# A two-layer convolution block on one core: four groups instead of three, with the last group kept on chip

## The chip, the cores and the metric

The kernel runs on one core of one Trainium2 chip. The metric is device time in microseconds, as the median of several runs of the whole kernel. A profile is one further execution with every engine's instructions, semaphores and DMA packets recorded. The engines are called PE (TensorE; PEld is its loading of weights), DVE (VectorE), ACT (ScalarE), POOL (GpSimd) and SP (the engine whose queue issues most DMAs here). ACTq, SPq and so on are the sequencers of these engines, which issue DMAs and wait.

## The reference

The input is 32 batches of 32 channels of 128x128 matrices in fp32. Two residual layers follow each other. `_gn` is a group norm over 16 groups of two channels.

```python
def layer0(A):                     # a matrix square root by iteration, for each of the 1024 matrices
    normA = sqrt(sum(A * A)); Y = A / normA; Z = I
    for _ in range(5):
        T = 0.5 * (3.0 * I - Z @ Y); Y = Y @ T; Z = T @ Z
    return Y * sqrt(normA)

def layer1(x, w1, w2):             # a spectral convolution
    X = fftn(x, axes=(2, 3)).real
    out = zeros
    out[:, :, :32, :32] = einsum('bixy,ioxy->boxy', X[:, :, :32, :32], w1)
    out[:, :, -32:, :32] = einsum('bixy,ioxy->boxy', X[:, :, -32:, :32], w2)
    return ifftn(out, axes=(2, 3)).real

x = x + layer0(_gn(x))
x = x + layer1(_gn(x), w1, w2)
```

## The kernel before, in words

**Layer 0 runs in sets.** A set is four channels of one batch, so a batch has 8 sets and there are 256. `newton` (L388) takes a set through its matrix products: `products` (L295, L298) makes four 128x128 products into one PSUM bank, `transposed` (L301, L304) makes four transposes on PE, `plus` (L270, L273) and `taken` (L262, L267) bring results out on DVE and ACT. At the end L410 adds the result to the input on DVE. There are two kinds of sets. For the far ones (batches 1 to 19, `is_far`, L307) `quartic` (L351) transposes by way of DVE and DRAM (L360 to L376); for the near ones (batch 0 and batches 20 to 31) it transposes on PE. Far sets may hold up to seven lanes at a time, near sets four, and a new set starts every 20/7 (far) or 13/4 (near) rounds (`LANES`, `LESS`, `FAR`, `NEAR`, L39 and L40).

**After a set** `settle` (L416) stores it to DRAM (`mid`, L418), folds its two halves on POOL (L423) and takes statistics on DVE (L427). After each four sets `forward` (L431) does the first transform. When a batch is complete, `spectrum` (L470) does the second transform (L479), then the group norm's statistics of the batch (`moments`, L493 to L516), then scales the spectrum (L521, L527) and stores it to DRAM (`xs`, L533).

**Layer 1 runs in groups of batches** (`GROUPS`, L41: 21, 8 and 3). When the last batch of a group has its spectrum, `follow` (L851) starts the products with the layer's weights for the whole group and puts the group's inverse transforms behind them. The first group uses `wide_products` (L540), where the weights stand on a diagonal in SBUF. Groups of at most eight use `small_products` (L596): the spectra are loaded onto the diagonal of two zeroed tiles (`diag0`, `diag1`, loads L617), the weights come in 16 steps of 512 KB (L611, L878), each step is 32 matmuls (L647), a pair of steps is copied out of PSUM (L662) and stored to DRAM (`od`, L626). A group with fewer than eight batches copies and stores four separate row ranges (`parts`, L600), alternately on ACT and DVE. `inverse` (L720) loads a batch's products (L683), reorders them on ACT for the small groups (`ob`, L730), transforms back on PE (L742, L764), copies parts on ACT (L748, L776), adds on DVE (L781) to the batch loaded from `mid` (L698), unfolds on POOL or in the tail partly on DVE (L717), and stores the output (L706).

**The order of work** is written out by hand: the loop at L868 makes rounds; in each round the lanes advance one stage and the generator queues `norms`, `preps`, `posts` (after a set), `specs` (spectra), `prods` (products) and `backs` (inverses) are stepped. `step` (L803) takes the first generator one stage on; when it has ended, it is removed and the next one waits for the next call. `backs` is stepped in four of five rounds, in every round once more than 26 batches have started to end. The framework that records the program orders each engine's instructions by its own priorities, except those wrapped in `kept`, which stay in program order; all engines execute in order.

**Tail.** `tail` is true when no set is left. Before, the tiles of the sets are then released (L875) and a pool `late` takes their place: 14 steps' weights for the last group are loaded there by POOL's queue (L878), and more room for `yt` tiles. Layer 0's buffers for far sets are given up once 20 batches have settled (`FIRST`, L50; `change`, L123), for the tiles of layer 1.

Of the kernel before, what the change touches and what calls it, by code (L numbers as in the profile page):

```python
# [26 lines left out]
F32 = mybir.dt.float32  # L28
# [12 lines left out]
GROUPS = (21, 8, 3)  # L41
# [8 lines left out]
FIRST = GROUPS[0] - 1  # L50
# [15 lines left out]
def conv_preact_kernel(  # L66
# [33 lines left out]
    for i, n in enumerate(GROUPS):  # L100
        few = n <= NB
        shape = [KK // 2, P, n, 64] if few else [KK, P, B, 32]
        xs.append(dram.tile(shape, F32, name=f"xs{i}", tag=f"xs{i}"))
        shape = [KK, 4, 32, 8 * C] if few else [KK, 4, B, L * C]
        od.append(dram.tile(shape, F32, name=f"od{i}", tag=f"od{i}"))
# [6 lines left out]
    phase = ctx.enter_context(ExitStack())  # L112
    sets = phase.enter_context(tc.tile_pool(name="sets", bufs=1))
# [356 lines left out]
    def spectrum(b, u, st):  # L470


        uv = u.rearrange("h s (t e l) c -> h s e t (l c)", e=2, l=4)
        ps = [bank() for _ in range(2)]
        for s in range(2):
            for i in range(2):
                for e in range(2):
                    rows = slice(64 * i, 64 * i + 64)
                    nc.tensor.matmul(  # L479
                        ps[i][64 * e : 64 * e + 64, 0:2, :],  # L480
                        tab[rows, T_FH.start + s * K : T_FH.start + (s + 1) * K],
                        uv[rows, s, e],
                        start=(s == 0),
                        stop=(s == 1),
                    )
        z = sp.tile([P, 4, P], F32, tag="sp", name="z", bufs=2)
        for i in range(2):
            nc.scalar.copy(
                z.rearrange("p t (l i c) -> p (t l) i c", i=2, c=G)[:, :, i, :],
                ps[i].rearrange("p a x -> p (a x)")[:, 0:256].rearrange("p (m c) -> p m c", c=G),  # L490
            )
        yield
# [23 lines left out]
        nc.vector.reciprocal(r, s)  # L516
        yield
        ps = transposed(z)
# [12 lines left out]
        i, j = where[b]  # L531
        kept(
# [63 lines left out]
    def small_products(i):  # L596

        n = GROUPS[i]

        parts = [slice(32 * q, 32 * q + 4 * n) for q in range(4)] if n < NB else [slice(0, P)]  # L600
        size = 4 * n * 64
        xks = [
            t[:, size * j : size * j + size].rearrange("p (b m) -> p b m", m=64)
            for t in diags
            for j in range(2048 // size)
        ]
        wts = [t.rearrange("p (e q t o) -> p e q t o", e=2, q=4, t=4) for t in plain] + late_wts

        def load_weights(kk):
            if kk < 2 or not late:  # L610
                kept(nc.sync.dma_start(out=wts[kk % len(wts)], in_=wk[kk]))  # L611

        def load_spectra(k2):
            for l4 in range(4):
                rows = slice(32 * l4, 32 * l4 + 32)
                kept(
                    nc.sync.dma_start(  # L617
                        out=xks[k2 % len(xks)][rows, n * l4 : n * l4 + n, :],
                        in_=xs[i][k2, rows, 0:n, :],
                    )  # L620
                )

        def store(k2, om):
            for rows in parts:
                kept(
                    nc.sync.dma_start(  # L626
                        out=od[i][2 * k2 : 2 * k2 + 2].rearrange("e q b x -> (q b) e x")[rows],
                        in_=om.rearrange("p (e x) -> p e x", e=2)[rows],
                    )
                )  # L630

        for t in diags:
            nc.gpsimd.memset(t, 0.0)
        for kk in range(2):
            load_weights(kk)
        for k2 in range(len(xks)):
            load_spectra(k2)
        done = None
        for kk in range(KK):
            yield  # L640
            k2, e = divmod(kk, 2)
            wt, xk = wts[kk % len(wts)], xks[k2 % len(xks)]
            if not e:
                pm = bank()
            for t in range(8):
                for q in range(4):
                    nc.tensor.matmul(  # L647
                        pm[32 * q : 32 * q + 4 * n, 2 * e + t // 4, 32 * (t % 4) : 32 * (t % 4) + 32],
                        xk[:, :, 32 * e + 8 * q + t],
                        wt[:, t // 4, q, t % 4, :],  # L650
                        start=True,
                        stop=True,
                    )
            if kk + len(wts) < KK:
                load_weights(kk + len(wts))
            if done and not e:
                store(*done)
            if e:
                om = page(f"om{i}_{k2}")[:, 0:512]
                for j, rows in enumerate(parts):  # L660
                    copy = nc.vector.tensor_copy if j % 2 else nc.scalar.copy
                    copy(om[rows], pm.rearrange("p a x -> p (a x)")[rows])  # L662
                done = k2, om
                if k2 + len(xks) < KK // 2:
                    load_spectra(k2 + len(xks))
        store(*done)
        yield

# [17 lines left out]
    def load_input(b, e):  # L686
# [4 lines left out]
        for i in range(2):  # L691
            o = 16 * e + 8 * i
            turn = len(yts) + i
            if late and turn % 2:
                y = late[0].tile([P, 8, P], F32, tag="yt_late", name=f"yt{b}_{o}", bufs=8)
            else:
                y = inv.tile([P, 8, P], F32, tag="yt", name=f"yt{b}_{o}", bufs=6)
# [105 lines left out]
    def step(queue):  # L803
        if queue and next(queue[0], queue) is queue:
            queue.pop(0)


    late = []
    late_wts = []
    lanes = [None] * LANES  # L810
# [19 lines left out]
    def end(b, g, xt):  # L830
# [6 lines left out]
        posts.append(settle(b, g, st, xt))  # L837
        if g % 4 == 3:
            posts.append(forward(b, g // 4, u))
        if g == C // 4 - 1:  # L840
            posts.append(last(b, u, st))

    def last(b, u, st):
        specs.append(spectrum(b, u, st))
# [23 lines left out]
    while todo or any(lanes) or posts or specs or prods or backs:  # L868
# [3 lines left out]
        if tail and not posts and not late:  # L872

            phase.close()
            late.append(ctx.enter_context(tc.tile_pool(name="late", bufs=1)))  # L875
            for kk in range(2, KK):
                late_wts.append(late[0].tile([P, 2, 4, 4, C], F32, name=f"wt{kk}_late"))
                nc.gpsimd.dma_start(out=late_wts[-1], in_=wk[kk])  # L878
        for i in range(LANES):
            step(norms)  # L880
            far = todo and is_far(todo[0][0])
            room = lanes[i] is None and (far or LANES - lanes.count(None) < LESS)
            if todo and room and rounds >= due:
# [6 lines left out]
                if stages:  # L890
                    stage()
            if lanes[i] is not None:
                b, g, xt, steps = lanes[i]
                if next(steps, lanes) is lanes:
# [10 lines left out]
            if i == 0 and (rounds % 5 or len(ended) > B - 6) or tail and not (posts or specs):  # L905
# [66 lines left out]
```

## Time and profile before

| what | us |
|---|---|
| median of 3 runs | 3214.82 |
| lowest and highest run | 3211.49 and 3221.01 |
| the profiled execution, its own time | 3217.96 |
| its span in the trace | 3216.0 |
| PE busy | 2973.3 |
| DVE busy | 2365.3 |
| POOL busy | 2008.4 |
| ACT busy | 1716.3 |

The span is from the first to the last record of the execution; its own time is measured from outside and has 1.96 us more. Busy time is the union of an engine's instructions. The page cuts the span in 40 slices and gives the busy share of each in tenths. Other views answer for a stretch of time: busy time of each engine, who waited for whom, the instructions in order of time, and the chain of work that ended last. Positions are microseconds from the start of the span. In the trace a matmul in fp32 with a moving operand has two records, a transpose has one; so `x64` on L647 is one step of 32 matmuls.

### The profile page before, as it was taken

The page shows a single profiled execution, that of the slowest core. Times are in us where ns is not written, and L with a number is a line of the kernel's source. Part 1 is how long each engine was busy: PE and PEld are TensorE (multiplying, and loading weights), DVE is VectorE, ACT ScalarE, POOL GpSimd, SP SyncE. Part 2 cuts the span into 40 slices and gives each one's busy share as a digit, 9 for nine tenths or more (in the row PEclk, how much of TensorE's full clock was granted, in tenths as well). Part 3 has the DMA queues.
Part 4 walks back from the last instruction along what each step waited for, and adds up shares of the span by engine and source line. Part 5 has one row for each costly group of instructions (what it writes and reads, how often), then busy time and mean ns, then how long its engine had stood idle before and what let it go on. Part 6 is the DMA issues. An engine that isn't in the chain of part 4 may idle for free.

```text
span 3216.0 us, 78946 instructions
## 1 busy us (share of the span) xinstructions
PE 2973.3 (92%) x29440; PEld 2836.6 (88%) x29440; DVE 2365.3 (74%) x5672; ACT 1716.3 (53%) x4148; POOL 2008.4 (62%) x2312
## 2 busy tenths in 40 slices
PE   6999999999999999999999999999999998999954
PEld 6889899899999999999999998898889888999853
DVE  5787788778888887888788665577767776756645
ACT  3555555565556655565565555455555544546533
POOL 3566666666767666666676553466767767746642
PEclk9999999999999999999999999999999999999975
DMA  3466566666666666666666336765767676576667
GB/s 122 148 190 190 192 201 202 186 199 204 196 208 200 210 191 196 207 204 200 191 211 193 96 96 207 227 214 185 232 201 243 213 240 208 193 225 209 207 238 255
DMA packets 482317, 637.55 MB, mean 198 GB/s; under 512 B 97936, under 2 KB 263056, under 8 KB 481936
## 3 DMA queue, kind: packets, MB, share of 16 engines
q1 hardware_dynamic: 366448, 413.30, 40.3%
q10 hardware_dynamic: 113472, 211.86, 21.1%
q0 software_dynamic: 2016, 7.34, 0.6%
q8 instruction: 235, 3.85, 0.5%
q14 instruction: 146, 1.20, 0.1%
HBM read 398.75 MB, written 233.57 MB: 197 GB/s over the span
## 4 chain that ended last, share of the span: by engine, by line
PE 67%; DVE 13%; DMA 12%; ACT 3%; issue 2%; POOL 1%; SPq 1%; ACTq 0%; DVEq 0%; POOLq 0%
PE ps L298 55%; PE ps L304 6%; DMA xs<-in_xt 5%; DMA turn<-turn 2%; PE ps L764 1%; DMA w<-turn 1%; DVE a_st L193 1%; PE ps L442 1%; DVE turn L360 1%; DVE q L273 1%; DVE yt L781 1%; DVE v L273 1%; PE ps L576 1%; PE ps L742 1%; DVE xt L410 1%
## 5 line engine op out<-in xcount | busy, mean ns | idle before, releaser
L298 PE MATMUL ps<-w,v 128*128 128x128 f32 x4096 | 548.5, 278 | 26.4 <-POOL w L376 14.1
L376 POOL TENSOR_TENSOR w<-w,r 128x512 f32<-128x512 f32 x304 | 386.7, 1275 | 270.5 <-DMA w<-turn 222.0
L298 PE MATMUL ps<-y,q 128*128 128x128 f32 x4096 | 549.6, 278 | 3.9 <-ACT y L267 2.2
L423 POOL TENSOR_TENSOR fold<-xt 128x256 f32<-128x256 f32 x512 | 363.7, 731 | 279.2 <-DVE xt L410 262.5
L328 ACT ACTIVATE b<-b,a_off,a_scr 128x128 f32<-128x128 f32 x1024 | 463.9, 489 | 129.7 <-issue 54.8
L298 PEld LDWEIGHTS ps<-w,v 128*128 128x128 f32 x4096 | 500.5, 193 | 35.2 <-POOL w L376 20.1
L298 PEld LDWEIGHTS ps<-y,q 128*128 128x128 f32 x4096 | 504.7, 194 | 7.0 <-ACT y L267 3.3
L273 DVE SCALAR_TENSOR_TENSOR q<-ps,eye 128x512 f32<-128x512 f32 x512 | 347.0, 678 | 99.5 <-PE ps L298 97.9
L717 POOL TENSOR_TENSOR yt<-yt,d 128x512 f32<-128x512 f32 x236 | 297.9, 1289 | 188.0 <-ACT d L776 155.0
L193 DVE BATCH_NORM_STATS2 a_st<-xs 128x6 f32<-128x128 f32 x1024 | 231.8, 279 | 143.4 <-DMA xs<-in_xt 143.0
L335 POOL TENSOR_SCALAR x<-xt,a_nm,a_sc 128x128 f32<-128x128 f32 x720 | 317.8, 454 | 23.9 <-DVE a_n L222 20.8
L404 ACT ACTIVATE y<-ps,a_t_s 128x128 f32<-128x128 f32 x1024 | 292.1, 369 | 62.3 <-PE ps L298 61.5
L292 POOL TENSOR_TENSOR r<-b,eye 128x512 f32<-128x512 f32 x104 | 132.8, 1277 | 283.8 <-issue 224.6
L298 PE MATMUL ps<-m,q 128*128 128x128 f32 x2048 | 280.3, 280 | 27.9 <-DVE q L273 27.6
L298 PE MATMUL ps<-m,mb 128*128 128x128 f32 x2048 | 282.4, 282 | 19.6 <-ACT mb L267 19.6
L273 DVE SCALAR_TENSOR_TENSOR v<-ps,x 128x512 f32<-128x512 f32 x256 | 175.5, 686 | 165.0 <-PE ps L298 162.9
L273 DVE SCALAR_TENSOR_TENSOR v<-ps,m 128x512 f32<-128x512 f32 x256 | 174.7, 683 | 162.8 <-PE ps L298 162.1
L298 PE MATMUL ps<-y,t 128*128 128x128 f32 x2048 | 280.6, 281 | 6.6 <-DVE t L273 4.5
L298 PEld LDWEIGHTS ps<-m,q 128*128 128x128 f32 x2048 | 252.1, 194 | 35.4 <-DVE q L273 17.9
L360 DVE STREAM_TRANSPOSE turn<-v 128x512 f32<-128x512 f32 x304 | 277.9, 914 | 7.2
L298 PE MATMUL ps<-x,b 128*128 128x128 f32 x2048 | 275.6, 278 | 5.6 <-POOL x L335 5.6
L298 PEld LDWEIGHTS ps<-m,mb 128*128 128x128 f32 x2048 | 254.9, 196 | 27.7 <-ACT mb L267 25.0
(124 smaller groups left out, 5867.6 us busy)
## 6 DMA issues: line engine op xcount, KB each, us to landing
turn<-turn SPq DMA_DIRECT2D x304, 256.0 KB
b<-in_x ACTq DMA_DIRECT2D x256, 256.0 KB
xt<-in_xt ACTq DMA_DIRECT2D x256, 256.0 KB
xs<-in_xt ACTq DMA_DIRECT2D x256, 256.0 KB
mid<-xt SPq DMA_DIRECT2D x256, 256.0 KB
yt<-mid SPq DMA_DIRECT2D x128, 512.0 KB
out<-yt SPq DMA_DIRECT2D x108, 512.0 KB
w<-turn SPq DMA_DIRECT2D x152, 256.0 KB
```

The costliest lines, as they stand in the source:

```text
L193: nc.vector.bn_stats(st[:, 4 * i + c, :], tiles[i][:, c, :])
L273: nc.vector.scalar_tensor_tensor(s, ps, f, t, ALU.mult, ALU.add)
L292: nc.gpsimd.tensor_tensor(r, mb, eye, ALU.add)
L298: nc.tensor.matmul(ps[:, j, :], lhsT[:, j], rhs[:, j], start=True, stop=True)
L304: nc.tensor.transpose(ps[:, j, :], t[:, j, :], ident)
L328: nc.scalar.activation(t, x, AF.Identity, bias=offset[:, c], scale=scale[:, c])
L335: nc.gpsimd.tensor_scalar(m[:, j, :], xt[:, j, :], nm[:, c // 2 : c // 2 + 1], sc[:, c : c + 1], ALU.add, ALU.mult,)
L360: nc.vector.transpose(blocks(t), v.rearrange(form, b=4))
L376: nc.gpsimd.tensor_tensor(w, w, r, ALU.add)
L404: nc.scalar.mul(y[:, j, :], py[:, j, :], sn[:, c : c + 1])
L423: nc.gpsimd.tensor_tensor(f[:, :, 64 * half : 64 * half + 64], xt[:, :, 0:64], xt[:, :, 64:128], op)
L717: engine.tensor_tensor(yh, yh, d, op)
```

## The change

The groups become 19, 8, 3 and 2, so batches 1 to 18 are far and 19 to 31 near. The group of three (batches 27 to 29) is treated before the last sets are through; the last group is batches 30 and 31. The last group (`own`) has no `xs` in DRAM: `spectrum` copies its scaled spectra straight onto the diagonal of `diag0` and `diag1`, in eight copies, four each on ACT and DVE. Those tiles are zeroed, and the weights of its first two steps loaded, at the end of the products of the group before. The other 14 steps' weights come as 28 half steps of 256 KB into tiles of the sets (tags b, x, xt, r, v, w) that the last sets no longer need; a generator `weights` issues them on SP once the last set has started, and after each stage of the last set and each settled set it can issue more. The pool `late` is gone; in the tail every third `yt` tile comes from the tag `fold`. In the last group four steps share one `om` page, so that there is half the number of stores, and the stores alternate between SP's and ACT's queue. The input of batch 30 is loaded at the start of its products.

The statistics of a batch become a generator of their own, `summed`, put ahead of the second `forward` of the batch. `step` goes on to the next generator in the same call when one has ended. `backs` is stepped in three of five rounds, and in every round once batch 31 has a set ended. Layer 0's far buffers are given up after 19 batches, the end of the first group.

```diff
-GROUPS = (21, 8, 3)
+GROUPS = (19, 8, 3, 2)
-FIRST = GROUPS[0] - 1
+FIRST = GROUPS[0]
...
-        xs.append(dram.tile(shape, F32, name=f"xs{i}", tag=f"xs{i}"))
+        if i < len(GROUPS) - 1:
+            xs.append(dram.tile(shape, F32, name=f"xs{i}", tag=f"xs{i}"))
...
+    def summed(b, st):
+        ms, _, d = yield from moments(st, "b")
...
+        scales[b] = v, r
+        yield
...
+        v, r = scales.pop(b)
         ps = transposed(z)
...
+        if i == len(xs):
+            n = GROUPS[i]
+            for e, t in enumerate(diags):
+                for l4 in range(4):
+                    rows = slice(32 * l4, 32 * l4 + 32)
+                    copy = nc.scalar.copy if l4 % 2 else nc.vector.tensor_copy
+                    copy(
+                        t.rearrange("p (k b m) -> p k b m", k=4, m=64)[rows, :, n * l4 + j, :],
+                        spec[rows, 8 * e : 8 * e + 8].rearrange("p (k e) q t -> p k (e q t)", e=2),
+                    )
+            yield
+            return
...
+            for j, rows in enumerate(parts):
+                queue = nc.scalar if own and j % 2 else nc.sync
                 kept(
-                    nc.sync.dma_start(
-                        out=od[i][2 * k2 : 2 * k2 + 2].rearrange("e q b x -> (q b) e x")[rows],
-                        in_=om.rearrange("p (e x) -> p e x", e=2)[rows],
+                    queue.dma_start(
+                        out=od[i][2 * k2 : 2 * k2 + held].rearrange("e q b x -> (q b) e x")[rows],
+                        in_=om[:, 0 : 256 * held].rearrange("p (e x) -> p e x", e=held)[rows],
                     )
                 )
...
+        held = 4 if own else 2
+        if not own:
+            for t in diags:
+                nc.gpsimd.memset(t, 0.0)
...
+        else:
+            for e in range(2):
+                load_input(B - n, e)
...
         store(*done)
+        if i == len(GROUPS) - 2:
+            for t in diags:
+                nc.gpsimd.memset(t, 0.0)
+            for kk in range(2):
+                load_weights(kk)
         yield
+
+    def weights():
+        kinds = [("b", 0)] * 5 + [("x", 0)] * 2 + [("b", 4)] + [("x", 4)] * 2
+        kinds += [("r", 9)] * 4 + [("v", 9)] * 3 + [("w", 9)] * 3
+        spent = 0
+        for half in range(4, 2 * KK):
+            while len(settled) - (B * C // 4 - 10) <= spent and (
+                not kinds or kinds[0][1] > len(stages_of_last)
+            ):
+                yield
+            if kinds and kinds[0][1] <= len(stages_of_last):
+                kind = kinds.pop(0)[0]
+            else:
+                kind = "xt"
+                spent += 1
+            t = four(kind, False)
+            late_wts.append(t)
+            kept(nc.sync.dma_start(out=t, in_=wk[half // 2, :, half % 2].rearrange("p q t o -> p q (t o)")))
+            yield
...
     def step(queue):
-        if queue and next(queue[0], queue) is queue:
+        while queue and next(queue[0], queue) is queue:
             queue.pop(0)
...
+        if g == C // 4 - 1:
+            posts.append(then(summed(b, st)))
         if g % 4 == 3:
             posts.append(forward(b, g // 4, u))
...
-        if tail and not posts and not late:
-            phase.close()
-            late.append(ctx.enter_context(tc.tile_pool(name="late", bufs=1)))
-            for kk in range(2, KK):
-                late_wts.append(late[0].tile([P, 2, 4, 4, C], F32, name=f"wt{kk}_late"))
-                nc.gpsimd.dma_start(out=late_wts[-1], in_=wk[kk])
...
-            if i == 0 and (rounds % 5 or len(ended) > B - 6) or tail and not (posts or specs):
+            if i == 0 and (rounds % 5 < 3 or len(ended) == B) or tail and not (posts or specs):
                 step(backs)
```

## The prediction

> **What bounds the kernel now.** I read the slices of the page first, then busy time by stretches, then the order of time after the last set of layer 0, then the chain for the price of single steps.
>
> The slices say where TensorE sets the pace and where it doesn't.
>
> ```profile
> span 3216.0 us, 78946 instructions
> PE   6999999999999999999999999999999998999954
> PEclk9999999999999999999999999999999999999975
> ```
>
> One slice is 80 us. TensorE is at nine tenths or more until the last two slices, where it is half idle and its clock falls. So there are two regimes. Until the last set of layer 0 ends (the last L410, at 3093.6) added TensorE work lengthens the span almost one for one; after it the time is a chain of hand-overs. The stretches give both their sizes (columns: stretch, length, then busy PE, PEld, DVE, ACT, POOL, then clock, DMA share, GB/s).
>
> ```profile
> 2100.00:2900.00 800.00, 751.68 (x7993) 712.12 (x7992) 572.18 (x1360) 405.59 (x989) 531.53 (x627) 0.98 0.65 214
> 2900.00:3093.60 193.60, 178.62 (x1792) 168.39 (x1794) 120.74 (x240) 105.86 (x237) 127.04 (x139) 0.97 0.65 202
> 3093.60:3109.00 15.40, 6.63 (x82) 4.55 (x74) 13.72 (x33) 6.93 (x16) 9.33 (x14) 0.80 0.90 300
> 3109.00:3127.90 18.90, 0.00 (x0) 0.03 (x1) 0.00 (x0) 0.00 (x0) 4.61 (x6) 0.50 0.91 357
> 3127.90:3167.10 39.20, 21.90 (x1088) 19.48 (x1088) 19.45 (x28) 12.86 (x26) 4.98 (x4) 0.59 0.58 184
> 3167.10:3181.20 14.10, 4.39 (x43) 4.10 (x46) 0.00 (x0) 3.93 (x4) 0.00 (x0) 0.50 0.80 216
> 3181.20:3211.40 30.20, 14.91 (x154) 13.09 (x153) 29.96 (x36) 12.03 (x30) 17.63 (x12) 0.56 0.96 337
> 3211.40:3216.00 4.60, 0.00 (x0) 0.00 (x0) 0.03 (x1) 0.00 (x0) 0.00 (x0) 0.50 0.57 228
> ```
>
> From 2900 to the last set TensorE idles 193.6 - 178.6 = 15.0 us. The tail is 122.4 us in six stretches, cut at events of the timeline:
>
> ```profile
> 3092.93 0.69 DVE L410 TENSOR_TENSOR xt<-ps,xt 128x512 f32<-128x512 f32 x1 [1.49 <-PE ps L298]
> ...
> 3109.02 0.37 SPq L533 DMA_DIRECT2D xs<-spec  x1
> ...
> 3127.90 1.90 PE L647 MATMUL ps<-plain,diag 128*12 128x32 f32 x128 [22.73 <-DMA diag<-xs]
> ...
> 3174.18 1.92 ACT L730 COPY ob<-or 128x1024 f32<-128x1024 f32 x1 [7.84 <-DMA or<-od]
> ```
>
> Spectrum of batch 31 (15.4), its way to DRAM and back (18.9, TensorE and VectorE idle), products (39.2, though TensorE works 21.9), products to DRAM, back and through the first transforms (14.1), three inverses in which VectorE is full (30.2), last stores (4.6).
>
> **What the Trainium skill says.** "DMA: Bandwidth & Descriptors", Anatomy of one DMA: a small transfer is mostly completion latency, about 2 us. The trace is worse: store and reload take 18.9 us, because the DMA share is 0.91 there (late weights and inputs run at the same time); so on-chip copies win the whole stretch. The same page, Issuing engines are not separate DMA queues: queues share 16 DMA engines, another queue saves issue time only. So moving the weights from POOL's queue to SP's changes no transfer, only who stands in line; an SP weight issue (L611) is 0.35 us. "TensorE: Matmul & The Clock Gate", Part 1: an idle array falls to half clock. The trace agrees (0.97 before the tail, 0.50 in the reload); I therefore leave the tail's matmuls at the tail's own rates.
>
> **The change, part by part.**
>
> *Tail, spectrum.* `summed` starts the statistics when the last set has settled, where before they stood behind `spectrum`'s matmuls and behind VectorE work of an inverse (L781 and L717, until about 3101.7). Timeline: last L410 to the u copies is 4.7 us (3093.6 to 3098.3). Then a short wait for the statistics 1.5, L479 1.1, z 0.7, transposes 1.1, spec 1.2, L527 0.2: 10.5 in place of 15.4. The instruction order has batch 29's VectorE adds before the last L410, so nothing else is in the way.
>
> *Tail, diagonal.* Eight copies of 32x256, four each on ACT and VectorE, replace store and load. No row has this form; ACT's 128x256 copy (L776) is 0.37, and "VectorE: DVE Perf Modes", The TRN2 errata, gives 224+256 cycles at 1.2 GHz = 0.40 us on ACT as an estimate. Side by side 1.5 us, one after another 3.2; I take 1.7, in place of 18.9. The memsets and the weights of the first two steps come earlier and are ready.
>
> *Tail, products.* In before each pair of steps waits on SP for a spectrum reload and four stores. After, no reloads, half as many stores on two queues. TensorE then sets the pace:
>
> ```profile
> 2864.72 1.07 PE ps L647 x63
> 2812.91 0.87 PE ps L304 x8
> 2946.52 1.09 PE ps L742 x16
> 2950.47 1.19 PE ps L764 x21
> ```
>
> (pieces of the chain: start, us). One step of products is 64 records, 1.07: 16 steps are 17.1. The last four copies alternate ACT and VectorE, 2.6 (3129.87 to 3132.50). 19.7 in place of 39.2; 22 if the copies of all eight pairs run one behind the other.
>
> *Tail, rest.* Products out and back I leave at 14.1 (12 to 16: both loads are issued at once, but share the queue). Two inverses instead of three, VectorE-bound at 30.2/3: 20.1. Last stores 4.6. The tail becomes 10.5+1.7+19.7+14.1+20.1+4.6 = 70.7; **saved 51.7** (46 to 58).
>
> *Main part, TensorE.* One more group means one more pass of products ahead of the last set: 17.1. Inverses are 32 either way; 30 are now done before the last set, where before it was 29 less half of one (L764 at 3099.7): 1.09+1.19+1.19 = 3.5, plus 1.2, together 4.7. Batch 19 changes from far to near: a near set transposes twice on TensorE (0.87, L304 x8) instead of by DMA; 8 sets are 7.0. Sum 28.8. If all 15 us of idle take some of it: 14; I take none, since those idle spots are late hand-overs that come with any inverse.
>
> *Main part, new waits.* (a) Group (27..29) has four separate row parts, so its copies alternate ACT, VectorE, ACT, VectorE (8 x 4) with work of the sets queued behind them on both engines; ACT stood 0.75 for each hand-over in the tail of before: 8 x 0.75 = 6 us of ACT, of which TensorE loses 0 to all; up to 12 if VectorE's queue is late. I take 2. (b) Three more inverses of small groups run before the last set (11 for 8), each with an ACT copy that waits for `or`: at 3003.93 that made TensorE wait 4.5 through sw; 0 to 13.5, I take 2. (c) 28 weight loads of 256 KB go onto SP during the last sets, each waiting for a tile of the sets: 28 x 0.35 = 10 us of issue, hidden unless SP stands; behind them are the mid stores of batch 31, the yt loads of 28 and 29 and the out stores. Value 0, see the last rival. (d) The loops that step a queue until it yields, and inverses in three rounds of five instead of four, change spacing, not work: 0, between -5 and +5. (e) The switch of buffers now falls with the end of the first group instead of a batch ahead of it; what may then stand on POOL is four memsets (2 x 1.8 and 2 x 0.96 us, L563), 0 to 5.5; the set that ends there leaves a round or more before products start: 0. The smaller first group leaves the wide products' matmuls as they are (the weights move, the batch axis is padded): 0. **Added: 28.8+2+2 = 33** (14 to 55).
>
> *Sum.* Profiled execution 3217.96 (span 3216.0 and 2 around it) - 51.7 + 33 = 3199.3. It lies 3.1 above the median 3214.82; the median forecast is **3196**.
>
> **Rivals.**
>
> *More gain.* The 15 us of idle are filled and (a), (b) cost nothing: added 14 to 20, time 3176 to 3182, say 3178. For: DVE and ACT are about 60% busy there. Against: TensorE idles there because of in-order waits, and those multiply with inverses.
>
> *No change.* The tail gains 46, the main part loses 28.8 + 6 + 10 = 45: 3214. For: the waits of ACT on `or` were long in before. Against: they need most of (a) and (b) on TensorE's path.
>
> *Slower.* One mechanism: SP's queue in the last 60 us before the last set. SP already stands long in before (waits of SP from 2985 to the end; who, for whom: total us, times, longest):
>
> ```profile
> SPq L418 <- DVE xt L410: 33.1, 5, 13.9
> SPq L698 <- DMA out<-yt: 13.7, 3, 8.2
> ```
>
> Now 28 loads stand among them, each held by a tile that is still read. If yt of batch 29 comes late by two or three waits of 13.9, VectorE, in order, holds q and w of the last sets: +28 to +42 on the forecast, about 3231. It decides once VectorE's waits for `yt<-mid` there add more than 19 us. Against: in the order the loads stand where their tiles' readers have been issued.
>
> **How the numbers follow.** Chances: forecast (3186 to 3205) 0.44, more gain 0.22, no change 0.17, slower 0.17. 0.3% is 9.6 us, about what runs of this kernel can tell from no change (they span 3211.5 to 3221.0). Below 3205.2: 0.66; above 3224.5: 0.17; between: 0.17. Ends: best bounds -58+14 give 3171, worst without the SP rival -46+55 give 3224; I stretch the upper end a little into it: 3170 to 3228.
>
> **What would show it.** Right: last L410 near 3126 of the new trace (3093.6+33), about 71 us after it; first small product 12 us after the last L410; products under 22 us; two inverses of 10 us. Wrong: first product over 20 us after it; products near 39 (SP or copies serial); last L410 above 3145, then the `om` copies, `or` or SP waits tell which. The forecast fails first if the main part grows by over 50 us.

## The result, and the profile after

The changed kernel takes 3244.88 us (median of 4 runs, 3239.81 to 3252.55), the kernel before 3214.93 on the same chip: ratio 1.0093, with a 95% interval of 1.0068 to 1.0118. It is slower by 30 us. The forecast was faster by 19.

The profiled execution of the changed kernel took 3239.81. In the new listing the lines have moved: L410 is L412, the products L647 are L680, the copies L662 are L699, the inverse's L742, L764, L776 and L781 are L806, L828, L840 and L845, and L717 is L781. First the slices of the changed kernel:

```profile
span 3238.0 us, 81144 instructions
PE   6999999999999999999999999999999998999984
PEclk9999999999999999999999999999999999999995
```

The two rows end in 84 and 95 where they ended in 54 and 75: the idle tail is shorter. Yet the span is 22.0 longer, so the loss is in the slices that look the same. (The two profiled executions are 22 apart and the medians 30; no trace here can show where the other 8 are.) The last L412 ends at 3153.5 where the last L410 ended at 3093.6. Busy time by stretches of the changed kernel, cut at the same events as before (columns: stretch, length, busy PE, PEld, DVE, ACT, POOL, clock, DMA share, GB/s):

```profile
2900.00:3153.50 253.50, 225.75 (x3024) 211.53 (x3024) 164.00 (x333) 127.77 (x295) 155.45 (x173) 0.96 0.71 230
3153.50:3167.56 14.06, 7.13 (x42) 4.04 (x43) 4.76 (x24) 4.32 (x10) 1.41 (x2) 0.52 0.62 236
3167.56:3199.48 31.92, 15.26 (x1024) 13.87 (x1024) 11.12 (x17) 9.56 (x18) 0.00 (x0) 0.50 0.12 19
3199.48:3213.66 14.18, 4.61 (x43) 4.32 (x46) 0.03 (x1) 4.95 (x4) 0.00 (x0) 0.50 0.75 227
3213.66:3233.58 19.92, 7.60 (x90) 6.73 (x88) 19.78 (x24) 6.01 (x18) 11.74 (x8) 0.59 0.39 158
3233.58:3238.00 4.42, 0.00 (x0) 0.00 (x0) 0.00 (x0) 0.00 (x0) 0.00 (x0) 0.50 0.59 237
```

| stretch | before | forecast | after |
|---|---|---|---|
| up to the last set | 3093.6 | 3126.6 | 3153.5 |
| spectrum and diagonal (before: and reload) | 34.3 | 12.2 | 14.1 |
| products | 39.2 | 19.7 | 31.9 |
| products out and back | 14.1 | 14.1 | 14.2 |
| inverses | 30.2 | 20.1 | 19.9 |
| last stores | 4.6 | 4.6 | 4.4 |
| tail in all | 122.4 | 70.7 | 84.5 |

So the tail gave 37.9 instead of 51.7, and the main part grew by 59.9 instead of 33. Three of the five rows of the tail came as forecast; one row, the products, carries nearly all of what is missing there.

**The products in the tail.** The chain of waits of the changed kernel in that stretch (start, us, what held it):

```profile
3166.47 0.21 DVE spec L536
3166.71 0.30 DVE diag L548
3167.02 0.29 DVE diag L548
3167.32 0.25 issue
3167.56 2.08 PE ps L680 x138
3169.64 1.55 issue
3171.19 1.90 PE ps L680 x128
3173.09 2.12 issue
3175.21 1.89 PE ps L680 x127
3177.10 1.74 issue
3178.84 1.90 PE ps L680 x128
3180.73 1.72 issue
...
3193.31 1.84 PE ps L680 x121
3195.17 0.58 ACT om L699
3195.78 0.68 DVE om L699
```

TensorE works 1.9 for 128 records and then stands 1.5 to 2.1 in "issue", time in which it waits for nothing that the profile shows; seven times, 12.3 in all. No weight, no page and no copy is late. Beside the stores, the view of transfers of the changed kernel from 3167 to 3200 has one line (packets, MB, share of 16 engines):

```profile
q8 instruction: 8, 0.13, 1.7%
```

Eight packets of 16,384 bytes on the queue of kind "instruction", at 3168.66, 3172.58, 3176.36 and so on, on average 3.67 apart, one for each block of 128 matmul records and their 128 weight loads: 256 records, so 64 bytes each if a record is an instruction. The reading is that TensorE used up its instructions faster than they came. That is a theory here; an experiment below tests it.

**The main part.** I summed TensorE's time up to the last set by line from the trace: its busy time, with overlaps counted once, and each idle spell put to the instruction after it.

| up to the last set | busy before | busy after | idle before | idle after |
|---|---|---|---|---|
| products of the layer (L647, L680) | 17.3 | 28.8 | 0.3 | 10.5 |
| inverses (L742 and L764, L806 and L828) | 96.4 | 106.2 | 0.0 | 7.2 |
| transposes of sets (L304, L306) | 262.9 | 270.7 | 35.8 | 21.4 |
| products of sets (L298, L300) | 2389.3 | 2398.9 | 93.8 | 113.2 |
| the rest | 159.7 | 158.3 | 38.2 | 37.5 |

Busy rose by 37.4, idle by 21.7, 59.1 in all of the 59.9. The executions of one kernel differ by more than 20 us (31 of the kernel before ran from 3195.0 to 3221.5), so a few microseconds in one row of one trace mean nothing; a row that grew by 10 and has a named wait means more. The products have one. TensorE's waits at them up to the last set, before, in the only pass of this kind:

```profile
PE ps L647 <- DMA od<-om: 0.3, 1, 0.3
```

and in the changed kernel, in the pass of the group of eight (2600 to 2760),

```profile
PE ps L680 <- DMA plain<-in_wk: 3.5, 2, 1.9
...
PE ps L680 <- DMA xt<-in_xt: 1.4, 1, 1.4
...
PE ps L680 <- issue: 0.8, 1, 0.8
```

and in the pass of the group of three (from 2760 on):

```profile
PE ps L680 <- DMA diag<-xs: 3.1, 1, 3.1
...
PE ps L680 <- DMA plain<-in_wk: 0.7, 1, 0.7
```

The third pass itself was cheaper than thought: its 16 steps keep TensorE busy for 12.1, which is 0.75 each, not 1.07. But both passes now wait for loads, and more than half of that is in the pass of the group of eight, which was there before.

In the last 110 us the waits of the changed kernel show one stall that the prediction had as its slower rival:

```profile
DVE yt L845 <- DMA yt<-mid: 9.4, 2, 8.9
...
PE ps L300 <- DVE q L275: 9.4, 2, 9.0
```

VectorE waits 8.9 for a `yt` of an earlier batch, and TensorE 9.0 for the `q` that stands behind it. The mechanism exists; it took place once, and 9.4 is half of the 19 from which it was to decide.

### The profile page after: what moved, and what is told of

Same layout as the page of the kernel before. It is cut to its first block, busy times and chain, and to the rows that moved or that the text cites. A ratio compares the mean times of both kernels' runs of the same rounds, so it can differ in the third digit from the quotient of the medians.

```text
span 3238.0 us, 81144 instructions
## 1 busy us (share of the span) xinstructions
PE 2997.5 (93%) x30528; PEld 2851.8 (88%) x30528; DVE 2364.5 (73%) x5684; ACT 1721.5 (53%) x4158; POOL 2001.0 (62%) x2312
## 5 line engine op out<-in xcount | busy, mean ns | idle before, releaser
L300 PE MATMUL ps<-w,v 128*128 128x128 f32 x4096 | 553.0, 279 | 35.9 <-POOL w L378 23.8
L378 POOL TENSOR_TENSOR w<-w,r 128x512 f32<-128x512 f32 x288 | 366.2, 1274 | 312.7 <-DMA w<-turn 204.8
L300 PE MATMUL ps<-y,q 128*128 128x128 f32 x4096 | 546.0, 277 | 2.5 <-ACT y L269 1.5
L300 PEld LDWEIGHTS ps<-w,v 128*128 128x128 f32 x4096 | 501.5, 193 | 49.2 <-POOL w L378 33.4
L300 PEld LDWEIGHTS ps<-y,q 128*128 128x128 f32 x4096 | 502.3, 194 | 4.7 <-ACT y L269 2.5
L781 POOL TENSOR_TENSOR yt<-yt,d 128x512 f32<-128x512 f32 x248 | 311.5, 1283 | 223.9 <-ACT d L840 193.9
L294 POOL TENSOR_TENSOR r<-b,eye 128x512 f32<-128x512 f32 x112 | 142.9, 1276 | 325.4 <-issue 249.8
L300 PE MATMUL ps<-m,q 128*128 128x128 f32 x2048 | 283.4, 282 | 23.5 <-DVE q L275 22.2
L300 PE MATMUL ps<-m,mb 128*128 128x128 f32 x2048 | 281.5, 281 | 21.3 <-ACT mb L269 21.3
L300 PE MATMUL ps<-y,t 128*128 128x128 f32 x2048 | 281.0, 281 | 16.8 <-DVE t L275 16.6
L269 ACT ACTIVATE mb<-ps 128x512 f32<-128x512 f32 x256 | 153.1, 598 | 264.7 <-PE ps L306 242.3
L300 PE MATMUL ps<-x,q 128*128 128x128 f32 x2048 | 278.1, 279 | 5.2 <-DVE q L275 3.9
L300 PEld LDWEIGHTS ps<-m,q 128*128 128x128 f32 x2048 | 254.5, 195 | 30.2 <-DVE q L275 24.5
L300 PE MATMUL ps<-x,b 128*128 128x128 f32 x2048 | 274.7, 277 | 6.5 <-POOL x L337 5.6
```

The lines of the kernel that those rows point to most:

```text
L269: nc.scalar.mul(t, ps, f)
L294: nc.gpsimd.tensor_tensor(r, mb, eye, ALU.add)
L300: nc.tensor.matmul(ps[:, j, :], lhsT[:, j], rhs[:, j], start=True, stop=True)
L378: nc.gpsimd.tensor_tensor(w, w, r, ALU.add)
L781: engine.tensor_tensor(yh, yh, d, op)
```

## The experiments

All are compared with the kernel before on the same chip, with the ratio and its 95% interval; 1% is 32 us. The changed kernel ran on one chip only, so where a run is compared with it, the ratios are compared. An edit that takes work away also moves what is left, so its price holds only as far as such moves cost little; more on that below. "Last set" is the end of the last L412 (L410 in kernels made from the one before).

**What the added work costs: take it away.** First the third pass of products, batches 27 to 29. Its weight and spectrum loads, matmuls and copies are left out, and its stores write a constant table, so three batches of the output have no products in them.

```diff
+            if n == 3:
+                return
...
-            for t in range(8):
+            for t in range(0 if n == 3 else 8):
...
-            if e:
+            if e and n == 3:
+                done = k2, tab
+            elif e:
```

> The changed kernel without the pass of products of the group of three: no weights, no spectra, no matmuls and no copies out of PSUM for batches 27 to 29, whose stores write a constant instead; everything else stays. By the prediction's price (17.1 of TensorE and 2 for the copies): 3226. Theory now (the pass also brings waits for spectra, weights and copies): 3215 to 3224. Rival (covered by idle TensorE): 3236 to 3245.

Measured 3216.48, ratio 1.0022 (1.0007 to 1.0036); the changed kernel's is 1.0093, so without the pass it is about 23 faster (28 between the two spans). The last set ended at 3124.6. In the table above the row of products grew by 21.7: 11.5 of work and 10.2 of waits. The size of the forecast (17.1 and 2 for copies) was nearly right, but for the wrong reason.

Then the near batch: one more batch made near, to price the one that the change made near.

```diff
-        return 0 < b < FIRST
+        return 0 < b < FIRST - 1
```

> The changed kernel with one more near batch: batch 18 is near too, nothing else changes. My prediction priced far to near at 7 us of TensorE a batch: 3252 (changed kernel 3245 + 7). Theory now (a near batch takes about 96 us where a far one takes 86, from the ends of sets in both traces, or up to 110 against 74 at the border): 3255 to 3280.

Measured 3250.99, 1.0124 (1.0098 to 1.0150): 6 (medians) to 10 (ratios) more than the changed kernel, with intervals that overlap. The 3255 to 3280 expected of a dear near batch did not come. The 7.0 of the forecast is not contradicted, and a near batch has no large hidden price.

Then the 28 half steps of weights on SP. They are left out, and the last group multiplies with the weights of its first two steps throughout, so the last two batches' output has wrong weights.

```diff
-            if own and kk >= 2:
+            if False:
...
-            t = four(kind, False)
-            late_wts.append(t)
-            kept(nc.sync.dma_start(out=t, in_=wk[half // 2, :, half % 2].rearrange("p q t o -> p q (t o)")))
+            late_wts.append(None)
```

> The changed kernel without the 28 loads of half steps' weights on SP's queue; the last group multiplies all 16 steps with the weights of the first two, so its numbers are not the reference's. Theory (the loads hold SP once, so that the input of batch 29 is late and VectorE waits 8.9 us): 3230 to 3240. Rival (the loads are the main cause of the loss in the main part): 3215 to 3228. Second rival (the loads are covered): 3242 to 3250.

Measured 3234.27, 1.0074 (1.0048 to 1.0101). By the ratios that is 6 less than the changed kernel, within the intervals; the last set came no earlier (3159.5, in an execution that was 12 longer than the median). In that trace the stall of 9 is gone: TensorE's waits for `q` in the last 110 us are 1.2 where they were 9.4. So the stall goes with the loads, but SP's queue is not where the 60 went.

**Is the tail's TensorE short of instructions?** The same weights in the last group with half the matmuls, each with twice the moving columns. The second of each pair of modes is thereby multiplied with the first one's spectrum.

```diff
-            for t in range(8):
+            w = 2 if own else 1
+            for t in range(0, 8, w):
...
-                        wt[t // 4][:, q, t % 4, :],
+                        wt[t // 4][:, q, t % 4 : t % 4 + w, :].rearrange("p t o -> p (t o)"),
```

> The changed kernel whose last group multiplies two modes' weights at a time with the first mode's spectrum: half the instructions, as many columns, so half its products are not the reference's. Theory F (in the tail TensorE runs dry of instructions: eight refills of 16 KB, 3.65 us apart, and 12.3 us of issue waits): four refills, products about 18 us instead of 32, time 3228 to 3234. Rival H (each pair of steps waits for the copies or the bank of the pair before): eight gaps stay, products 29 to 32 us, time 3242 to 3247.

Measured 3233.14, 1.0073 (1.0039 to 1.0107). By the ratios the whole time is only 6 lower, with intervals that overlap; in its trace the main part ends 10 later (3163.9). The tail is what it was made for, and it is 72.6 instead of 84.5. By stretches, to the last copy and to the first add of an inverse:

```profile
3178.03:3198.00 19.97, 9.44 (x512) 8.90 (x512) 10.96 (x17) 9.58 (x18) 0.00 (x0) 0.84 0.18 27
3178.03:3212.15 34.12, 14.04 (x555) 13.21 (x558) 10.97 (x18) 14.52 (x22) 0.00 (x0) 0.70 0.42 110
```

and in its waits (total, times, longest):

```profile
PE ps L681 <- issue: 3.0, 2, 1.8
```

Half the instructions, the same weights, pages, copies and stores: four instruction packets instead of eight, at the same distance (3.56), the waits of "issue" fall from 12.3 to 3.0, and from the first product to the first add it is 34.1 instead of 46.1. The packets set the pace: the theory stands. The granted clock differs too (0.84 here, 0.50 there), but the distance of the packets does not follow it. Why a packet takes that long is not shown. What is left of the stretch then is the copies behind one another.

**Does the order cost, without any work?** Beginning from the kernel before, only the statistics ahead (`summed`) and the new `step` were put in. No work is added, groups and pacing are those of before.

```diff
-        if queue and next(queue[0], queue) is queue:
+        while queue and next(queue[0], queue) is queue:
...
+        if g == C // 4 - 1:
+            posts.append(then(summed(b, st)))
```

> The kernel before with only the order edits of layer 1's statistics: summed ahead of the second forward, and a queue that goes on to its next generator in the same call. Theory (these edits cost nothing; the main part is lost to the third pass of products, to one more near batch and to the weight loads on SP's queue): 3208 to 3220, as before (3215). Rival (the order edits crowd the main part): 3225 to 3240.

Measured 3244.18, 1.0103 (1.0078 to 1.0128): as much as the whole change. A part of that is work moved forward: with the new `step` one and a half inverses more are done ahead of the last set (1856 records of them against 1760), 13 of busy and idle time there, and the tail is 7.6 shorter. The last set comes 30 later (3123.8). I split the edit. The new `step` for the three kinds of queue in turn (here for the inverses; the others change the name):

```diff
+        while queue and next(queue[0], queue) is queue:
             queue.pop(0)
+            if not (queue is backs):
+                break
```

> The kernel before, in which only the queue of work after a set (posts) goes on to its next generator in the same call. Theory A (the 35 us of the order edits come from inverses that follow each other more closely, six calls instead of seven): 3205 to 3215, as before. Theory B (they come from folds, statistics and forward transforms that enter the instruction order earlier, in a lump with the sets): 3230 to 3245.

> The kernel before, in which only the queue of inverses (backs) goes on to its next generator in the same call, so that an inverse takes six calls instead of seven. Theory A (closer inverses crowd the sets): 3230 to 3245. Theory B (the posts are the cause): 3205 to 3215.

> The kernel before with the new step for all queues, and the statistics left inside the spectrum. If the step is the cause, 3235 to 3250 as with both order edits; if it is the statistics put ahead of the second forward, 3205 to 3218.

For what follows a set (first): 3205.92, 0.9997 (0.9975 to 1.0018), nothing. For the inverses (second): 3226.87, 1.0052 (1.0030 to 1.0075). For all queues (third): 3221.04, 1.0039 (1.0021 to 1.0056). So `step` is worth 12 to 17 on the kernel before, and the statistics about 20 more. If that were the price of the statistics, the changed kernel without them would gain it back: its statistics were put back into `spectrum`.

```diff
-    def summed(b, st):
+    def spectrum(b, u, st):
...
-        if g == C // 4 - 1:
-            posts.append(then(summed(b, st)))
```

> The changed kernel with the statistics back inside the spectrum, behind its transform; all else stays. Theory S (statistics ahead of the second forward put a wait for VectorE in front of TensorE's work in every batch, some 20 us in 32 batches as the two runs on the kernel before suggest): 3220 to 3232, although the tail gets about 5 us longer. Theory R (no single order edit costs anything of its own; each edit gives another interleaving of the sets, good or bad by some 10 to 15 us): anything from 3230 to 3260.

Measured 3258.46, 1.0169 (1.0143 to 1.0195): 24 slower than the changed kernel. The theory that the statistics have a price of their own fell: the same edit costs 20 on one kernel and saves 24 on the other. The tail, expected to be 5 longer, is the same (84.7 and 84.5).

Perhaps any moved order does that. In the kernel before I moved one call by four places in the round, the one that prepares the next batch:

```diff
-            if i == 1:
+            if i == 5:
```

> The kernel before with the preparation of the next batch (preps) stepped after the sixth lane of a round instead of the second: same instructions, same number of calls, another interleaving. Theory S: no change, 3205 to 3215. Theory R: it moves by 8 us or more in either direction.

Measured 3239.99, 1.0102 (1.0075 to 1.0129). An edit that adds no work costs 33, as much as the change under study; here as many inverses as before are done ahead of the last set (1760 records). In its waits from 2100 to the last set VectorE waits longer for its inputs,

```profile
DVE a_st L193 <- DMA xs<-in_xt: 76.0, 26, 5.8
```

where the same line before has

```profile
DVE a_st L193 <- DMA xs<-in_xt: 56.0, 25, 7.3
```

To see whether a late preparation is bad in itself, the same on the changed kernel, and beside it a move of the spectra:

```diff
-            if i == 1:
+            if i == 5:
```

> The changed kernel with the preparation of the next batch stepped after the sixth lane of a round instead of the second, the same edit that made the kernel before 1% slower. Theory R (interleaving is luck, the kernel before has a good one and the changed kernel may have an ordinary one): between 0.990 and 1.006 of the changed kernel's 1.0093, in either direction. Theory P (late preparation always delays the next batch's loads): 1% slower again, 1.018 to 1.022 against the kernel before.

```diff
-            if i == 2 or tail:
+            if i == 4 or tail:
```

> The changed kernel with the spectra's queue (specs) stepped after the fifth lane instead of the third. Theory R: differs from the changed kernel by 5 us or more in either direction. If only some edits matter (preps), no difference: 1.007 to 1.012 against the kernel before.

The first: 3243.22, 1.0107 (1.0080 to 1.0133), no different from the changed kernel, so in that kernel it isn't. The second: 3253.88, 1.0144 (1.0111 to 1.0177), some 16 slower, with intervals that just overlap. Last, the two order edits of the change that were left, undone on the changed kernel: the pacing of inverses, and `step` for all queues but those after a set.

```diff
-            if i == 0 and (rounds % 5 < 3 or len(ended) == B) or tail and not (posts or specs):
+            if i == 0 and (rounds % 5 or len(ended) > B - 6) or tail and not (posts or specs):
```

> After with one line put back: inverses are stepped in four rounds of five (in every round once more than 26 batches have started to end), as before. If the denser spacing of three in five costs a part of the main stretch (step d of the prediction, put at -5 to +5), the time falls by 8 to 20 us against after, to 3225 to 3237, ratio 1.003 to 1.007, and the last set ends near 3135 to 3145 instead of 3153.5. If the order is only shuffled anew, anything between -15 and +20 against after is possible with no sign favoured. If the spacing costs nothing: 3240 to 3250, last set near 3153.

```diff
         while queue and next(queue[0], queue) is queue:
             queue.pop(0)
+            if not (queue is posts):
+                break
```

> After with the step that goes on to the next generator kept only for the queue of what follows a set; specs, products and inverses are stepped as before (one call for an ended generator). On the kernel before, the change of step for the inverses alone cost about 17 us and for the posts alone nothing. If these costs carry over, the time falls by 10 to 20 us against after, ratio 1.003 to 1.006. If they don't carry over between kernels, within 8 us of after or slower, ratio 1.007 to 1.013.

Pacing: 3241.38, 1.0112 (1.0088 to 1.0137), no difference; the last set ended at 3152.5. `step`: 3257.20, 1.0161 (1.0133 to 1.0190), 22 slower than the changed kernel, although its last set came at 3112.8; its inverses were left for the tail. Undoing an edit that costs 12 to 17 on the kernel before costs here. Of five edits of order alone on each kernel (some contain others) none made it faster beyond its interval; they cost 0 to 33 before and 0 to 24 after.

**Other versions.** If the third pass is the trouble, drop it: groups of 22, 8 and 2 (far batches then up to 21), with inverses in four rounds of five and twice a round at the end; then the same with the statistics in `spectrum`.

```diff
-GROUPS = (19, 8, 3, 2)
+GROUPS = (22, 8, 2)
...
-            if i == 0 and (rounds % 5 < 3 or len(ended) == B) or tail and not (posts or specs):
+            if i == 0 and (rounds % 5 or len(ended) > B - 6) or i == 3 and len(ended) > B - 2 and not prods or tail and not (posts or specs):
```

> The changed kernel with groups of 22, 8 and 2: three groups, so no third pass before the last set, and three batches fewer near; inverses are stepped in four of five rounds as before, and twice a round at the end. From the runs: minus 25 (the pass), minus 3 times 6 to 10 (near batches), plus up to 10 for inverses that crowd the last two batches: 3195 to 3215 where the changed kernel has 3245. If the crowding of inverses decides, 3220 to 3240.

> As groups of 22, 8 and 2, with the statistics back inside the spectrum. Theory S: 10 to 20 us below that run, less 5 for the longer tail. Theory R: within 15 us of it in either direction. One inverse more is left for the tail, which is 10 us.

Measured 3235.61, 1.0095 (1.0072 to 1.0117), and 3255.17, 1.0163 (1.0123 to 1.0202). The pass is gone and the last set comes at 3136.2 and 3131.1, but the tail is 90.7 and 107.0; nothing is won. (The executions of the second lie 41 us apart, so its 20 more than the first are rough.) The rival of crowded inverses shows in the first: TensorE's idle ahead of inverses up to the last set is 35 where the changed kernel has 7.2.

Then the kernel before with only what shortens its tail: in the last group of three, the first eight steps' spectra go onto the diagonal on chip, tiles are zeroed and first weights loaded after the pass ahead, four steps share a page, stores alternate between two queues. Groups and order stay. The second kernel has the pages and the stores alone.

```diff
+        if i == len(GROUPS) - 1:
+            n = GROUPS[i]
+            for e, t in enumerate(diags):
+                for l4 in range(4):
...
-                    nc.sync.dma_start(
-                        out=od[i][2 * k2 : 2 * k2 + 2].rearrange("e q b x -> (q b) e x")[rows],
+                    queue.dma_start(
+                        out=od[i][2 * k2 : 2 * k2 + held].rearrange("e q b x -> (q b) e x")[rows],
...
+        held = 4 if n < NB else 2
```

> The kernel before with edits to its last group alone: the spectra of batches 29 to 31 for the first eight steps are put on the diagonal on chip, their tiles zeroed and the first weights loaded after the pass before, four steps share one page and the stores alternate between two queues. Groups, near and far, pace and step stay. Theory R (the tail's means are worth their time, and what the change loses is the third pass and the interleaving of the main part): tail 100 to 110 us instead of 122, ratio 0.992 to 0.998. Rival (any edit that puts copies into the last batches costs the main part 10 to 30 us): ratio 1.000 to 1.008.

> The kernel before with only the stores of the last group edited: four steps share one page and the stores alternate between SP and ACT. The main part's instructions stay as they are. Products of the tail 32 to 36 us instead of 39, ratio 0.997 to 1.000; if the main part's interleaving moves although nothing in it was edited, 1.003 or more.

Measured 3197.31, 0.9972 (0.9955 to 0.9989), and 3203.20, 0.9979 (0.9963 to 0.9995). By the ratios the first beats both kernels, by 9 and by some 39 us, but the two cannot be told apart, and the tail explains little: from the last set to the end it is 113.1 with the diagonal (3072.5 to 3185.6; 100 to 110 was expected) and 121.9 with the stores alone, where before it was 122.4. With the diagonal the products begin 16.1 after the last set instead of 34.3, but then take 47.4 instead of 39.2. The chain of the first says why:

```profile
3087.99 15.60 DMA xs<-spec
3104.09 1.31 SPq L628
...
3108.12 2.45 DMA diag<-xs
```

The other eight steps still go through DRAM: their store takes 15.60 to land, and the reload stands on SP's queue behind it. In the stores' kernel the products take 38.8, not the 32 to 36 expected: TensorE's "issue" is there too.

```profile
PE ps L649 <- issue: 13.3, 6, 4.2
```

Why it is nonetheless 7 faster than the kernel before is open.

## Why the prediction was wrong, point by point

The forecast for the profiled execution was 3199.3. The tail saved 13.8 less than forecast, the main part grew by 26.9 more, and 0.2 is less around the span: 3239.8. First the tail.

*Right: what the tail would no longer do.* Store and reload gone (34.3 became 14.1, forecast 12.2), out and back 14.2 (14.1), two inverses 19.9 (20.1), last stores 4.4 (4.6). The eight copies onto the diagonal took 0.415 each on ACT and 0.275 on DVE, 1.7 side by side, as forecast; the prediction's estimate of 0.40 for ACT, worked out from the Trainium skill ("VectorE: DVE Perf Modes", The TRN2 errata), fits. The gain is that of the copies: putting the statistics ahead brings only about 1 here (first product 14.1 after the last set, and 15.1 with the statistics back in `spectrum`), and from the last set to the copies it is 13.0 where 10.5 was taken. The 2 us that the prediction quotes for a small transfer stand in "DMA: Bandwidth & Descriptors", Anatomy of one DMA, for transfers that POOL issues; this store and reload were SP's, and no sum of the prediction uses the 2.

*Wrong size: "TensorE then sets the pace", 19.7.* It did, but at 31.9. The price of a step, 1.07, came from a row of the main part, where a step's 64 records are spread among other work, although the prediction meant to leave the tail's matmuls at the tail's own rates. In the tail 16 steps follow one another, and 128 records with their weight loads need 16 KB of instructions, which come every 3.67 on average. The trace of before had it: TensorE's waits in its tail list

```profile
PE ps L647 <- issue: 12.9, 5, 5.6
```

and the prediction did not read it; it took all of TensorE's standing there for SP's waits, to vanish with them. 12.2 lost; shown by the halved instructions.

Now the main part, term by term (busy and idle time of TensorE from the table above, both kernels up to the last set):

| term | forecast | measured |
|---|---|---|
| third pass of products and (a), its copies | 19.1 | 21.7 |
| inverses and (b), their waits | 6.7 | 17.0 |
| sets: batch 19 near, and (d), the order | 7.0 | 22.4 |
| the rest, and the two ends | 0 | -1.2 |
| in all | 33 | 59.9 |

*Third pass and (a): right in size,* but made of 11.5 of work and 10.2 of waits, most of them for loads, which the prediction did not name. It put SP's loads at 0 because only issue was counted. The copies of (a) did alternate (DVE waits for ACT at L699), and TensorE lost little to it.

*Wrong size: the inverses, 4.7.* By records, 28 first and 27.3 second transforms were done before the last set (448 of 16 each, 1312 of 48), and 30 of each now. The prediction counted one and a half inverses where it was 2 and 2.7. Busy rose 9.8.

*Right mechanism, too small: wait (b).* TensorE's idle ahead of inverses rose by 7.2 where 2 were taken. A line of the waits from the end of batch 27 to the last set has most of it:

```profile
PE ps L806 <- ACT ob L794: 6.5, 2, 3.4
```

It lies inside the range of 0 to 13.5 given for it.

*The near batch, 7.0:* transposes are busy 7.8 longer, and one more near batch cost 6 to 10.

*The step that failed: (d), "change spacing, not work: 0, between -5 and +5".* It is the largest of the three wrong sizes. The row of the sets grew by 15 more than the near batch's 7.0: set products and transposes, whose number is as forecast, are busy 10 longer and wait 5 longer. Edits of order alone moved the two kernels by 0 to 33 us, so -5 to +5 was never a bound. The prediction took added TensorE work to lengthen the span one for one, and with it that the sets would fit into one another as well as before. What is shown is that order alone can cost as much as this change does. That these 15 are the sum of the three order edits of the change is not shown: 15 is within what executions of one kernel differ by, and undone one by one on the changed kernel, two of the edits (statistics, `step`) make it slower and one (pacing) does nothing. No price of one carries over from kernel to kernel. So the cause of the 15 stays open, and no single step turned the sign: the forecast gain was 18.7, and 12 at the tail's products, 10 at the inverses and 15 at the sets were lost together.

*One thing that goes with it.* TensorE's granted clock falls to 0.50 for 3.4 to 10.2 us at a time in the midst of the main part, with TensorE busy. In the changed kernel eight records of a set's product took 1.16 at 3092.31 and 2.08 at 3145.26, inside such a stretch. Up to the last set such stretches add up to 82 us in the kernel before (TensorE busy in 74) and 109 (97) in the one with late preparation; if busy time doubles there, that is by estimate 12 of the 30 by which its last set comes later. Of 43 executions of the kernel before on one chip the 13 with a mean clock of 0.971 or less took 3216.0 on average, and the 8 with 0.975 or more 3198.6. Whether the clock or the waits come first is not shown, and in the changed kernel they add up to 75 (66), so its 15 are not explained by this.

*The rivals.* "Slower" had the right sign and the wrong place: SP's loads cost one stall of 9, and without them 6 are gained within the noise. "No change" needed added work of 45, "more gain" 20 at most; it was 60.

## What to carry to other kernels

Price a step of many small matmuls from a stretch in which such steps follow one another, and read "issue" waits in the stretch that you mean to speed up before you put them down to the wait that you remove: here 12 us of them stayed. Where in-order engines interleave two streams of work by a hand-made order, treat each edit of that order as a term of unknown sign of up to 1% of the span (here up to 33 us of 3215), and prefer changes that leave it alone. Count instances of work by records up to the cut, not by the schedule you believe in.

## What the hardware showed that I had not expected

TensorE's instructions came in packets of 16,384 bytes, one for 256 records of matmuls and weight loads, and in the tail's products, where nothing longer is mixed in, a packet came every 3.67 us on average, and every 3.56 with half the instructions. 128 records with 32 moving columns were done in 1.9 us even at a clock of 0.50, so TensorE was busy 15.3 of 31.9 us; with 64 columns the same stretch needed half the packets, and the granted clock in it was 0.84. In the changed kernel's pass of the group of eight packets came 4.2 to 9.3 us apart, and TensorE waited for "issue" 0.8 us in all.
